# Layer 2 of a four-layer graph network: row sums behind out's kept sum, statistics of x behind the keys' store, loads of x written a block sooner

## The chip, the core and the metric

The kernel runs on one core of a Trainium2 chip. A core has five engines that run side by side, each with its own queue of instructions: TensorE (PE in the profile) multiplies matrices, VectorE (DVE), ScalarE (ACT) and GpSimd (POOL) do elementwise work, and SyncE (SP) issues the transfers between the large memory and the core's on-chip buffers. An engine takes its instructions in the order in which they stand; where an operand is not ready, the engine waits. The metric is the device time of one execution in microseconds (us).

## The reference, cut to what matters

128 graphs of 64 nodes with 512 features pass four layers of the form x = x + layer(relu(layernorm(x))). The change is in layer 2, which is attention over the nodes of one graph with 8 heads of 64 features, its scores multiplied by twice the adjacency:

```python
def layer2(x, adj, Wq, bq, Wk, bk, Wv, bv, Wo, bo):
    h = maximum(layernorm(x), 0)
    q, k, v = (heads(h @ W.T + b) for W, b in ((Wq, bq), (Wk, bk), (Wv, bv)))
    scores = einsum('bhqd,bhkd->bhqk', q, k) * 64 ** -0.5
    attn = softmax(scores * (adj + adj), axis=-1)
    ctx = einsum('bhqk,bhkd->bhqd', attn, v)
    return x + merged(ctx) @ Wo.T + bo
```

Layer 1 adds its value bias to x; the kernel leaves that to the beginning of layer 2, where each block of x gets `b1v` added once.

## The kernel before

All 8192 tokens are cut into 32 blocks of 256 tokens (`T`), four graphs each. Layers 0 and 1 run interleaved, two blocks at a time, and write x to the large memory as `x1`; layer 2 then runs over all blocks and writes `x2`; layer 3 runs last. All arithmetic is 32-bit floating point. Every product of a block with a 512x512 weight matrix is made by a Strassen-like scheme (`Product`) of seven products of halves instead of eight. The class gathers them in two PSUM banks, `ab` and `dc`, in two steps: four products in `first` and `second`, three in `late`. Between the steps the intermediate sums must be saved, because the late products are added to the same banks: `keep_ab` copies `a` on ACT (`p1`) and adds `b + p1` on DVE (L281, the kept sum `u2`, `self.kept`), and `keep_dc` copies `c` on ACT (`p5`). PE can't start the late products on `ab` before the kept sum is made. The sums of halves of the input that the scheme needs are made on POOL by `sums` (L216 to L219: S1, S2, S4, S3).

One block of layer 2 takes these steps. `prepare2` loads x and the adjacency, adds `b1v` (L906), and calls `norm`: statistics on DVE (L167, L168, L170), the power -1/2 on POOL (L172), a last factor on DVE (L174) and the normalised h on ACT (L179). `turned2` transposes h on PE (L190); DVE and ACT copy it out (L195, L193). `layer2_in` makes q and k side by side, and `store_T` writes them with their bias (L310, L313, L319 on DVE, L323 on ACT, L326 on POOL). `layer2_scores` makes the scores (L642) and on DVE the product with the adjacency (L652), the row maximum (L661) and the difference (L662), then the exponential on ACT (L665), the row sums and their reciprocals on DVE (L667, L668), and the division as a multiplication on POOL (L669). `layer2_turned` transposes e on PE (L682), `layer2_context` multiplies it with v (L703) and adds the value bias, giving cT (L711 on DVE, L716 on ACT). `out_part` makes the sums of cT and the last product, which `add_to` adds to x (L335 to L342).

The loop over blocks is written as a software pipeline: in iteration b stand the products q and k of block b + 1, then the context and the last product of block b, with the scores of block b + 1 between. `prepare2(b + 2)` is called in the middle.

The order on each engine is not that of the text alone. A scheduler goes through the program with an estimate of its own and issues what it takes to be ready, the earlier in the text first; it also decides when a buffer's slot is free. `tc.issue_after(ins)` tells it not to issue the instructions inside before `ins`. The pools set how far it can run ahead: x has 4 slots, the adjacency 3, h 6, the exponentials 3. `behind[0]` is an instruction on POOL behind which the chores are put. A chore (L99) is one of the sums of weight quarters for a coming product (1.3 us each), spread over the blocks.

Of the kernel before, what the change touches and what calls it, by code (L numbers as in the profile page):

```python
# [25 lines left out]
def kernel(ctx: ExitStack, tc: tile.TileContext, a: dict, out: bass.AP):  # L26
# [7 lines left out]
    nc = tc.nc  # L34
    x_d, adj_d, adjT_d = a["x"], a["adj"], a["adjT"]
    n_tok = x_d.shape[0]
    n_blk = n_tok // T
# [164 lines left out]
    behind = [None]  # L202

    def sums(hT, name: str, places=("S", "S")):

        A11, A12, A21, A22 = (
            hT[:, j * 2 : (j + 1) * 2, i * P : (i + 1) * P] for i in range(2) for j in range(2)
        )
        (S1, S2), (S3, S4) = (
            (s[:, 0], s[:, 1])  # L210
            for s in (
                med.tile([P, 2, 2, P], FP, tag=tag, name=f"S{i}_{name}", bufs=6 if tag == "S" else 3)
                for i, tag in enumerate(places)
            )
        )
        nc.gpsimd.tensor_tensor(S1, A21, A22, ALU.add)  # L216
        nc.gpsimd.tensor_tensor(S2, S1, A11, ALU.subtract)
        nc.gpsimd.tensor_tensor(S4, A12, S2, ALU.subtract)
        behind[0] = nc.gpsimd.tensor_tensor(S3, A11, A21, ALU.subtract)  # L219
        return {1: (A11, B11), 4: (A22, T4), 5: (S1, T1), 6: (S2, T2),  # L220
                2: (A12, B21), 3: (S4, B22), 7: (S3, T3)}

    class Product:
# [84 lines left out]
        def store_T(self, y, bias):  # L308

            nc.vector.tensor_tensor(self.u3, self.b, self.p1, ALU.add)  # L310
            for m in range(2):
                f = slice(m * P, (m + 1) * P)
                nc.vector.scalar_tensor_tensor(  # L313
                    y[:, m, P:], self.d[:, f], bias[:, m : m + 1], self.u3[:, f],
                    ALU.add, ALU.add,
                )
            for m in range(2):
                f = slice(m * P, (m + 1) * P)
                nc.vector.scalar_tensor_tensor(  # L319
                    y[:, 2 + m, :P], self.c[:, f], bias[:, 2 + m : 3 + m], self.u2[:, f],  # L320
                    ALU.add, ALU.add,
                )
                nc.scalar.activation(  # L323
                    y[:, m, :P], self.a[:, f], AF.Identity, bias=bias[:, m : m + 1]
                )
            nc.gpsimd.tensor_tensor(  # L326
                y[:, 2:, P:],
                self.u3.rearrange("p (m q) -> p m q", m=2),
                self.p5.rearrange("p (m q) -> p m q", m=2),
                ALU.add,  # L330
            )
# [266 lines left out]
    def setup2():  # L598
# [5 lines left out]
            later(w)  # L604
        return made

    def layer2_in(b: int, hT, between=()):

        ops = sums(hT, f"2_{b}")
        qk = big.tile([P, 2, K, T], FP, tag="qk", name=f"qk_{b}")  # L610
        side_by_side(*(
            (ops, w, bias, lambda p, i=i, bias=bias: p.store_T(qk[:, i], bias), f"{'qk'[i]}2_{b}")
            for i, (w, bias) in enumerate(zip(made1[5], (b2q, b2k)))
        ), between=between)
        return qk, ops
# [12 lines left out]
    def layer2_scores(b: int, adjq, qk):  # L628

        ss = [
            ps_sc.tile([P, TT, hq // 2, 2, N], FP, tag="sc", name=f"s2_{b}_{o}") for o in range(2)
        ]
        for t in range(TT):
            for c in range(hq):
                for g in range(2):
                    tok = slice(t * P + g * N, t * P + (g + 1) * N)
                    for par in range(2):
                        f = slice(par * N, (par + 1) * N)  # L640
                        half = par ^ (c % 2)
                        nc.tensor.matmul(  # L642
                            ss[c % 2][half * N : (half + 1) * N, t, c // 2, g, :],
                            qk[f, 0, c, tok], qk[f, 1, c, tok],
                            start=True, stop=True,
                        )
        es = []
        for o in range(2):

            e = med.tile([P, TT, hq // 2, 2, N], FP, tag="e2", name=f"e2_{b}_{o}", bufs=3)  # L650
            eh = e.rearrange("p t c g j -> p (t c g) j")
            nc.vector.tensor_tensor(  # L652
                e.rearrange("p t c g j -> p t c (g j)"),
                ss[o].rearrange("p t c g j -> p t c (g j)"),
                adjq.rearrange("p t g j -> p t (g j)")
                .unsqueeze(2)
                .to_broadcast([P, TT, hq // 2, 2 * N]),
                ALU.mult,
            )
            mx = small.tile([P, TT * hq], FP, tag="mx2", name=f"mx2_{b}_{o}")  # L660
            nc.vector.tensor_reduce(mx, eh, AX.X, ALU.max)  # L661
            nc.vector.tensor_tensor(  # L662
                eh, eh, mx.unsqueeze(2).to_broadcast([P, TT * hq, N]), ALU.subtract
            )
            nc.scalar.activation(e, e, AF.Exp, scale=0.25)  # L665
            r = small.tile([P, TT * hq], FP, tag="r2", name=f"r2_{b}_{o}")
            nc.vector.tensor_reduce(r, eh, AX.X, ALU.add)  # L667
            nc.vector.reciprocal(r, r)  # L668
            nc.gpsimd.tensor_tensor(  # L669
                eh, eh, r.unsqueeze(2).to_broadcast([P, TT * hq, N]), ALU.mult  # L670
            )
            es.append(e)
        return es

    def layer2_turned(b: int, es):
        pTs = []
# [220 lines left out]

    loaded2, normed2 = {}, {}

    def prepare2(b: int):  # L900
        if b < n_blk:
            loaded2[b] = load_x(b, x1[b], 2), load_adjq(b)

            for t in range(TT):
                x = loaded2[b][0]
                nc.vector.tensor_tensor(x[:, t, :], x[:, t, :], b1v, ALU.add)  # L906
            normed2[b] = norm(x, f"2_{b}")
# [13 lines left out]
    next(setup)  # L921
    open_end = []
    for i, (layer, b) in enumerate(steps):
        if i == 1:
            made1 = next(setup)
        between = [[], [chore], []]
        for n, end in open_end:
            between[n].append(end)
        if i + 1 < len(steps):
            between[0].append(lambda: prepare(i + 1))  # L930
            between[2].append(lambda: turned(i + 1))
        else:
            between[0].append(lambda: prepare2(0))
            between[2].append(lambda: turned2(0))
        if layer == 0:
            softmax = layer0(b, *loaded[b], *normed[i], between)
            open_end = [(0, lambda b=b, softmax=softmax: layer0_end(b, *softmax))]
        else:
            attention = layer1(b, *loaded[b], *normed[i], between)
            open_end = [  # L940
                (1, lambda b=b, a=attention: layer1_end(b, loaded[b][0], *a, x1[b]))
            ]
        if i == len(steps) - 3:
            made2 = setup2()

# [30 lines left out]
    coming = values(0, ops)  # L976
    next(coming)
    es = layer2_scores(0, loaded2[0][1], qk)
    v = next(coming)
    chore(2)  # L980
    for i in (2, 1):
        w3[i] = fetched(f"L3_Wk{i}", 1 + i, nc.sync)
        later(w3[i])
    for b in range(n_blk):
        x = loaded2[b][0]
        with tc.issue_after(behind[0].ins):
            for t in range(TT):
                nc.gpsimd.tensor_tensor(x[:, t, :], x[:, t, :], made2[1], ALU.add)
        stages = iter(())
        if b == n_blk - 2:  # L990
            stages = layer3_in(0, *normed3, made_in)
            next(stages)
        if b + 1 < n_blk:
            qk, ops = layer2_in(b + 1, normed2[b + 1], [[], [lambda: chore(1 if b else 2)]])
        else:
            parts = layer3_step(0, False)
            next(parts)
            chore(2)
        if b == n_blk - 2:
            w3[0] = fetched("L3_Wk0", 4, nc.sync)  # L1000
            later(w3[0])
        pTs = layer2_turned(b, es)
        if b + 1 < n_blk:
            prepare2(b + 2)
            coming = values(b + 1, ops)
            next(coming)
        else:
            next(parts)
        cT = layer2_context(b, v, pTs)
        part = out_part(b, x, cT)  # L1010
        if b + 1 < n_blk:
            es = layer2_scores(b + 1, loaded2[b + 1][1], qk)
            v = next(coming)
            turned2(b + 2)
            next(stages, None)
        else:
            next(parts)
        side_by_side(part)
        chore(2 if b == n_blk - 2 else 0)
        nc.sync.dma_start(tokens(x2[b]), x)  # L1020
        if b == n_blk - 4:
            made3 = setup3()
        if b >= n_blk - 3:
            normed3 = layer3_norm(b - n_blk + 3, x2[b - n_blk + 3])
# [69 lines left out]
```

## Time and profile before

| what | us |
|---|---|
| median of three runs | 2693.18 |
| lowest and highest of them | 2690.39 and 2693.68 |
| the profiled execution | 2690.4 |
| its span, from the first to the last instruction | 2688.6 |
| layers 0 and 1 | 0 to about 1026 |
| layer 2, from its first q to the last out | about 1020 to 1990 |
| layer 3 | about 1960 to the end |

The span is what all lines of the trace refer to; 1.8 us lie around it. A line of a timeline gives the start, the duration, the engine, the line of the code, the operation, the output and the inputs, and how many equal instructions it merges; in brackets is the idle time of the engine before it and what ended this idle time. Durations of matmuls are modelled with their way through the pipeline and overlap, so the distance from one start to the next is what counts there. A line of the costliest groups gives the count, then the busy time, the mean of one in nanoseconds, and the idle time before. In a table of stretches the columns are the stretch, its length, and the busy time and count of PE, of the weight loads, of DVE, ACT and POOL, then PE's granted clock, the transfers' share and GB/s.

### The profile page before, as it was taken

The numbers are of one execution on the slowest core, as the hardware profiler recorded it, in microseconds if no ns is written. First come the engines' busy times: TensorE is split into PE (matmuls) and PEld (weight loads), VectorE is DVE, ScalarE is ACT, GpSimd is POOL, SyncE is SP. The second block draws the span as 40 slices with busy tenths as digits, with TensorE's granted clock in tenths as the row PEclk, the third lists the DMA queues.
The fourth block names the chain that finished last, engine by engine and source line by source line (L and its number), as shares of the span: only waits on it lengthen the run. The fifth ranks groups of instructions, "written<-read, shape, count | busy, mean of one in ns | idle before, by whom it ended". The sixth has DMA issues, their size and how long they took to land.

```text
span 2688.6 us, 52721 instructions
## 1 busy us (share of the span) xinstructions
PE 2646.6 (98%) x20752; PEld 2256.7 (84%) x20752; DVE 1682.3 (63%) x4398; ACT 942.7 (35%) x2290; POOL 1274.9 (47%) x1585
## 2 busy tenths in 40 slices
PE   8999999999999999999999999999999999999999
PEld 5888888888888888898999999999877777777776
DVE  5566666666666666555655655555666666666664
ACT  2333334333433333333333333333323333333332
POOL 3443333333334344655654565555564544444454
PEclk9999999999999999999999999999999999999999
DMA  4200111111101112111111111111211111111110
GB/s 155 69 35 34 34 34 35 42 43 37 47 34 34 34 66 78 37 52 37 39 45 44 39 37 52 37 39 52 72 50 46 56 51 51 51 51 51 51 50 32
DMA packets 103165, 129.81 MB, mean 48 GB/s; under 512 B 40834, under 2 KB 50050, under 8 KB 102916
## 3 DMA queue, kind: packets, MB, share of 16 engines
q1 hardware_dynamic: 102340, 125.38, 14.0%
q8 instruction: 163, 2.67, 0.4%
q10 hardware_dynamic: 576, 1.05, 0.1%
q14 instruction: 86, 0.70, 0.1%
HBM read 76.07 MB, written 50.34 MB: 47 GB/s over the span
## 4 chain that ended last, share of the span: by engine, by line
PE 77%; DVE 11%; DMA 5%; POOL 3%; ACT 2%; issue 2%; POOLq 0%; SPq 0%; ACTq 0%; DVEq 0%
PE ab_v L251 10%; PE ab_y L251 10%; PE dc_v L251 8%; PE dc_y L251 7%; PE ab_g L244 4%; PE ab_g L251 4%; DMA x<-x 4%; PE dc_g L244 3%; PE ab_q L244 3%; PE dc_g L251 3%; PE ab_k L244 3%; PE po L392 3%; PE tr L190 3%; PE dc_k L244 2%; PE dc_q L244 2%; DVE e L662 2%
## 5 line engine op out<-in xcount | busy, mean ns | idle before, releaser
L179 ACT ACTIVATE h<-x,nmr,rstd 128x512 f32<-128x512 f32 x256 | 194.4, 806 | 212.7 <-DVE nmr L174 208.8
L167 DVE BATCH_NORM_STATS2 stats<-x 128x6 f32<-128x512 f32 x256 | 167.3, 675 | 75.4 <-DMA x<-x 71.1
L172 POOL TENSOR_TENSOR rstd<-ve,neghalf 128x2 f32<-128x2 f32 x128 | 89.5, 699 | 260.8 <-DVE ve L170 260.5
L251 PE MATMUL ab_y<-L_Wk,hT 128*128 128x256 f32 x768 | 206.2, 391 | 3.6 <-DVE u_y L303 2.6
L251 PE MATMUL ab_v<-L_Wv,hT 128*128 128x256 f32 x768 | 202.8, 387 | 4.8 <-DVE stats L167 3.7
L251 PEld LDWEIGHTS ab_y<-L_Wk,hT 128*128 128x128 f32 x768 | 136.1, 190 | 75.9 <-issue 25.1
L251 PE MATMUL ab_v<-L_Wv,S 128*128 128x256 f32 x768 | 198.0, 381 | 0.0
L251 PE MATMUL ab_y<-L_Wk,S 128*128 128x256 f32 x768 | 197.9, 380 | 0.0
L251 PE MATMUL dc_v<-L_Wv,S 128*128 128x256 f32 x768 | 197.3, 380 | 0.0
L251 PE MATMUL dc_y<-L_Wk,S 128*128 128x256 f32 x768 | 193.8, 381 | 0.2 <-DVE u_y L851 0.2
L251 PEld LDWEIGHTS dc_y<-L_Wk,S 128*128 128x128 f32 x768 | 146.2, 191 | 21.4 <-DVE u_y L851 1.7
L251 PEld LDWEIGHTS ab_v<-L_Wv,S 128*128 128x128 f32 x768 | 146.8, 191 | 19.9
L872 POOL TENSOR_TENSOR tz<-tz,y 128x512 f32<-128x512 f32 x63 | 91.3, 1449 | 146.1 <-ACT tz L869 146.1
L251 PEld LDWEIGHTS dc_v<-L_Wv,S 128*128 128x128 f32 x768 | 143.8, 191 | 18.8 <-issue 0.8
L251 PEld LDWEIGHTS ab_y<-L_Wk,S 128*128 128x128 f32 x768 | 144.1, 191 | 18.1
L251 PEld LDWEIGHTS ab_v<-L_Wv,hT 128*128 128x128 f32 x768 | 136.5, 191 | 22.9 <-ACT qk L323 7.5
L190 PE MATMUL tr<-ident,h 128*128 128x128 f32 x1024 | 134.3, 275 | 0.4 <-ACT h L179 0.4
L190 PEld LDWEIGHTS tr<-ident,h 128*128 128x128 f32 x1024 | 119.4, 142 | 11.2 <-ACT h L179 0.8
L216 POOL TENSOR_TENSOR S<-hT 128x256 f32<-128x256 f32 x128 | 100.8, 788 | 38.4 <-ACT hT L193 36.0
L326 POOL TENSOR_TENSOR qk<-u_q,p_q 128x256 f32<-128x256 f32 x32 | 23.3, 727 | 195.5 <-DVE u_q L310 195.5
L281 DVE TENSOR_TENSOR u_v<-ab_v,p_v 128x256 f32<-128x256 f32 x96 | 40.6, 423 | 109.7 <-ACT p_v L280 109.7
L219 POOL TENSOR_TENSOR S<-hT 128x256 f32<-128x256 f32 x128 | 107.0, 836 | 1.2
(238 smaller groups left out, 6472.6 us busy)
## 6 DMA issues: line engine op xcount, KB each, us to landing
x<-x SPq DMA_DIRECT2D x128, 512.0 KB, 3.4
x<-in_x_dram SPq DMA_DIRECT2D x32, 512.0 KB, 3.5
out_dram<-x SPq DMA_DIRECT2D x31, 512.0 KB, 2.8
adjT<-in_adjT_dram SPq DMA_DIRECT2D x64, 64.0 KB, 1.9
adjq<-in_adj_dram SPq DMA_DIRECT2D x64, 64.0 KB, 2.3
L_Wk<-in_L_Wk_dram SPq DMA_DIRECT2D x16, 256.0 KB, 5.2
L_Wv<-in_L_Wv_dram SPq DMA_DIRECT2D x12, 256.0 KB, 5.1
q<-in_L_Wqk_dram ACTq DMA_DIRECT2D x4, 256.0 KB, 5.4
```

The source lines that it names most:

```text
L167: nc.vector.bn_stats(stats[:, t, :], x[:, t, :])
L172: nc.gpsimd.tensor_tensor(rstd, ve, neghalf, ALU.pow)
L179: nc.scalar.activation(h, x[:, t, :], AF.Relu, bias=nmr[:, t : t + 1], scale=rstd[:, t : t + 1])
L190: nc.tensor.transpose(pt[:, k, :], h[:, k * P : (k + 1) * P], ident)
L216: nc.gpsimd.tensor_tensor(S1, A21, A22, ALU.add)
L219: behind[0] = nc.gpsimd.tensor_tensor(S3, A11, A21, ALU.subtract)
L244: nc.tensor.matmul(dst[:, m * P : (m + 1) * P], w[:, place, k, m * P : (m + 1) * P], left[:, k, :], start=key not in self.begun, stop=last ...
L251: nc.tensor.matmul(dst, left[:, k, :], w[:, place, k, :], start=key not in self.begun, stop=last and k == 1, skip_group_check=True,)
L281: self.kept = nc.vector.tensor_tensor(self.u2, self.b, self.p1, ALU.add)
L392: nc.tensor.matmul(ps[t][half[g ^ t]], e[half[g], t, :], us[t][half[g]], start=True, stop=True)
L662: nc.vector.tensor_tensor(eh, eh, mx.unsqueeze(2).to_broadcast([P, TT * hq, N]), ALU.subtract)
L872: nc.gpsimd.tensor_tensor(tz[t], tz[t], y0[:, t, :], ALU.add)
```

## The change

Three groups of edits, all in the order of layer 2's work; no instruction is added or removed.

*Row sums.* The row sums, their reciprocals and the multiplication leave `layer2_scores` and become `layer2_divided`. For block 0 it is called directly behind the scores. For the others it is called behind the last product, and nothing of it is issued before that product's kept sum.

*Statistics and sums.* `store_T` keeps two of its instructions: `taken`, the last of its DVE instructions (L319), and `stored`, the addition on POOL (L326). `prepare2(b + 2)` is issued after `taken` of the keys of block b + 1. In `layer2_in` the sums of a block are issued after `stored` of the keys of the block before (for block 0, after `behind[0]`), and after block 0's scores `behind[0]` is set to its `stored`.

*Loads.* The loads of x and of the adjacency move from `prepare2` to `fetch2`, which is called one block sooner: `fetch2(b + 3)` beside `prepare2(b + 2)`, and for blocks 0 to 2 within the last steps of layers 0 and 1.

```diff
-                nc.vector.scalar_tensor_tensor(
+                self.taken = nc.vector.scalar_tensor_tensor(
                     y[:, 2 + m, :P], self.c[:, f], bias[:, 2 + m : 3 + m], self.u2[:, f],
...
-            nc.gpsimd.tensor_tensor(
+            self.stored = nc.gpsimd.tensor_tensor(
                 y[:, 2:, P:],
...
+    of_qk = {}
+
     def layer2_in(b: int, hT, between=()):
 
-        ops = sums(hT, f"2_{b}")
+        with tc.issue_after((of_qk[b - 1][1].stored if b else behind[0]).ins):
+            ops = sums(hT, f"2_{b}")
         qk = big.tile([P, 2, K, T], FP, tag="qk", name=f"qk_{b}")
-        side_by_side(*(
+        of_qk[b] = side_by_side(*(
...
             nc.scalar.activation(e, e, AF.Exp, scale=0.25)
+            es.append(e)
+        return es
+
+    def layer2_divided(b: int, es):
+
+        for o, e in enumerate(es):
+            eh = e.rearrange("p t c g j -> p (t c g) j")
             r = small.tile([P, TT * hq], FP, tag="r2", name=f"r2_{b}_{o}")
             nc.vector.tensor_reduce(r, eh, AX.X, ALU.add)
             nc.vector.reciprocal(r, r)
             nc.gpsimd.tensor_tensor(
                 eh, eh, r.unsqueeze(2).to_broadcast([P, TT * hq, N]), ALU.mult
             )
-            es.append(e)
-        return es
...
+    def fetch2(b: int):
+        if b < n_blk:
+            loaded2[b] = load_x(b, x1[b], 2), load_adjq(b)
+
     def prepare2(b: int):
         if b < n_blk:
-            loaded2[b] = load_x(b, x1[b], 2), load_adjq(b)
...
+        if i == len(steps) - 2:
+            fetch2(0)
...
         else:
+            fetch2(1)
             between[0].append(lambda: prepare2(0))
...
+            if b == n_blk - 2:
+                open_end.append((1, lambda: fetch2(2)))
...
     es = layer2_scores(0, loaded2[0][1], qk)
+    layer2_divided(0, es)
     v = next(coming)
+    behind[0] = of_qk[0][1].stored
...
         if b + 1 < n_blk:
-            prepare2(b + 2)
+            with tc.issue_after(of_qk[b + 1][1].taken.ins):
+                prepare2(b + 2)
+            fetch2(b + 3)
...
-        side_by_side(part)
+        (of_o,) = side_by_side(part)
+        if b + 1 < n_blk:
+            with tc.issue_after(of_o.kept.ins):
+                layer2_divided(b + 1, es)
```

## The prediction, made before the changed kernel had run

> **What bounds the kernel now.** I read the page's busy table first, then the sums over stretches, then the timelines of TensorE, DVE and POOL inside layer 2.
>
> ```profile
> span 2688.6 us, 52721 instructions
> PE 2646.6 (98%) x20752; PEld 2256.7 (84%) x20752; DVE 1682.3 (63%) x4398; ACT 942.7 (35%) x2290; POOL 1274.9 (47%) x1585
> ...
> 1061.42:1826.05 764.63, 754.06 (x8114) 699.12 (x8113) 431.52 (x1058) 263.73 (x674) 425.44 (x527) 1.00 0.13 42
> ```
>
> PE sets the time: it never rests long, so only what removes a PE wait counts. The stretch holds 26 blocks of layer 2, 764.63 / 26 = 29.41 us each. An undisturbed block (transposes of e at 1417.31 to those at 1446.41) takes 29.10, so 764.63 - 26 x 29.10 = 8.0 us are occasional stalls. Inside every block there is one more, at out's late products:
>
> ```profile
> 1429.98 1.03 PE L251 MATMUL dc_o<-L_Wo,cT 128*128 128x256 f32 x4
> 1430.84 0.38 PE L244 MATMUL dc_q<-S,L_Wq 128*128 128x128 f32 x2
> 1431.43 1.13 PE L251 MATMUL ab_o<-L_Wo,cT 128*128 128x256 f32 x4 [0.21 <-DVE u_o L281]
> 1432.40 1.03 PE L251 MATMUL ab_o<-L_Wo,S_c 128*128 128x256 f32 x4
> ...
> 1428.33 1.26 DVE L667 TENSOR_REDUCE r<-e 128x8 f32<-128x512 f32 x2
> 1429.52 0.31 DVE L668 RECIPROCAL r<-r 128x8 f32<-128x8 f32 x2
> ...
> 1430.97 0.41 DVE L281 TENSOR_TENSOR u_o<-ab_o,p_o 128x256 f32<-128x256 f32 x1
> ```
>
> Read starts, not durations. Two dc_q matmuls fill in and are worth 0.22 (8 take 0.89), so PE should go on at 1431.06, but starts at 1431.43: 0.37 lost. Its first group then takes 0.97 to the next start where others take 0.87: 0.10 more. It waits for the kept sum u_o, which ends at 1431.38, behind the row sums on DVE. The occasional stalls begin with a load of x, and the entry into layer 2 has its own:
>
> ```profile
> 1090.09 1.29 DVE L906 TENSOR_TENSOR x<-x,L_bv 128x512 f32<-128x512 f32 x2 [4.74 <-DMA x<-x]
> ...
> 1093.02 1.13 PE L251 MATMUL ab_v<-L_Wv,hT 128*128 128x256 f32 x4 [1.46 <-DVE stats L167]
> ...
> 1044.13 0.48 PE L642 MATMUL s<-qk 64*64 64x64 f32 x16 [3.54 <-POOL qk L326]
> 1044.54 2.01 PE L251 MATMUL ab_v<-L_Wv,hT 128*128 128x256 f32 x4
> 1046.35 1.87 PE L251 MATMUL ab_v<-L_Wv,S 128*128 128x256 f32 x4
> 1048.05 1.03 PE L251 MATMUL dc_v<-L_Wv,S 128*128 128x256 f32 x4
> ```
>
> DVE stands at L906 for a load that has just been issued; everything behind it on DVE (storing q and k) is late, and in turn PE. At the entry the last store of k (L326) sits on POOL behind four sums of the next block and a weight chore (1038.50 to 1042.91).
>
> [...] after the 3.54 us wait two groups take 1.81 and 1.70 from start to start, against 0.97 and 0.87, 1.67 us on top. [...] L218, which meets the subtraction L662, takes half as long again as L217.
>
> ```profile
> L218 POOL TENSOR_TENSOR S_c<-cT,S_c 128x256 f32<-128x256 f32 x32 | 35.4, 1106 | 2.4
> L217 POOL TENSOR_TENSOR S_c<-S_c,cT 128x256 f32<-128x256 f32 x32 | 23.3, 727 | 0.0
> ```
>
> **The change part by part.** I compared the order in which the two built programs' instructions stand on each engine. PE's order differs only in the filler: it moves behind out's late products, its work unchanged. SP's order is the same but for single places at the entry and exit. In the old order too the load of x(n+4) follows the store of x(n), because the scheduler had pulled loads and statistics ahead of the written order. So the loads do not come sooner. What changes is their use: beside the products q, k of block 12 stood the bias and statistics of x(14), now x(13), whose load was issued a block (29 us) earlier.
>
> *Loads' wait.* The load takes 2.8 us behind the store plus some 3.5 us; with 29 us to spare no wait remains: -8.0. Bounds: 0 (another cause) and -8.0. I take -8.0: the longest stalls, at 1093.02, 1212.07, 1359.83 and 1477.27, all name the statistics L167, with L906 held by the DMA before them.
>
> *Entry.* The sums of block 1 now follow the stores of q and k on POOL, and L906 of x(2), x(3) with their statistics are off DVE there. The k store can run at about 1036 and the scores' last 16 matmuls follow the first 48. Gain 3.54 + 1.67 = 5.2. What is late next: POOL then does two chores (1.27 each) and two additions of bo (1.25 each), 5.0 us, so S1 of block 1 is there at 1041.8; PE, 3.5 us earlier, asks at 1043.4. Bounds -3 and -5.6; I take -5.2.
>
> *Row sums behind the kept sum.* 1.26 + 0.31 us leave DVE's path to u_o. They cost nothing later: DVE next waits for out's late products (2.09 us before L337 in a neighbouring block), and the multiplication on POOL, now behind L336, ends near 5 us after out's late start, where the transposes of e come at 15.1. The price is behind it on POOL: L338, L342 and the store of x come about 1 us later; its load has a block to spare. Full gain 0.37 + 0.10 = 0.47 less the rounding in the sum below: PE's block without the wait is 14 groups of L251 at 0.866, 14 of L244 at 0.893, two transposes at 0.875, 0.98 and 1.11 for the 64-wide products and 0.19 for two switches = 28.66, that is 0.44 less than 29.10.
>
> *Statistics behind the keys' store.* This adds a chain that must end inside the block. Time from out's late start: dc_k ends 15.10; DVE stores k until 16.35 (L313 follows by 0.21, then 2 x 0.52); L906 1.22, two L167 1.20, aggregates, u_v (0.33) and ve: 19.5; POOL's power and nmr 1.0: 20.4. The v sum u_v lies in this queue: 19.25, needed at 21.6. h on ACT 20.6 to 22.0; the transposes want it at 24.3: 2.3 spare. But cT's four activations now queue behind h: they end at 23.2, where they were done 1.4 us after pc and are now 2.7 after. POOL's sums of cT begin at 23.2, the third (S2) ends at 25.3 undisturbed and, as it now meets L662 (from 24.0), up to 26.2. PE needs S2 at 26.06. L662 ends at 26.5 instead of 25.9, u_o at 28.5, needed at 28.66. So the block is closely fitted: a new wait of 0 to 0.35 per block. I take 0.1, so 0.33 x 28 blocks = -9.2; bounds -12.3 and +2.
>
> *Exit.* Bias and statistics of x(31) (L906, L167: 2.4 us) and of layer 3's first block (another 1.5) now share one block, ahead of cT on DVE, and one L780 (0.68) stands before u_o: 1 to 1.5 us late once or twice. I take +2, bounds 0 and +4.
>
> Sum: -8.0 - 5.2 - 9.2 + 2 = -20.4. The profiled execution took 2690.4 (span 2688.6 and 1.8 around it), so 2670.0. The median of the three runs is 2693.2, 2.8 above it, which I count into the range.
>
> **Rivals.** (1) *Tight fit takes the steady gain*: S2 or u_o late by 0.4 in each block. For: a gap of only 0.1 to 0.8 us by my working. Against: today's S2 is done 1.9 us before its use. -8.0 - 5.2 + 0 + 2 = -11.2: 2679. (2) *No new wait at all and a clean exit*: -8.0 - 5.2 - 12.3 + 0 = -25.5: 2665. (3) *The loads' stalls stay*, as SP's order is unchanged: -5.2 - 9.2 + 2 = -12.4: 2678. Against: the block that is used is another. (4) *Slower*: the chain k store, statistics, h, cT, S2 ends late in every block and PE waits at ab_o<-S_c. It decides from 25.5 - 2 = 23.5 us over 28 blocks = 0.84 us of wait per block; at 1.2 us it gives +10: 2700. For: all four engines stand in this chain[...]. Against: my sum would have to be wrong by 0.8 us or more.
>
> **How the numbers follow.** Forecast (2664 to 2675) 0.50; rival 2 beyond it 0.09; rivals 1 and 3 together (2675 to 2685) 0.26; between that and no change 0.06; slower 0.09. A difference under 0.2% (5.4 us) can hardly be told from no change here. The range leaves out the slow cases and the far end of rival 2: 2662 to 2684. Faster 0.86, same 0.05, slower 0.09.
>
> **What would show it.** Right: the wait of ab_o for u_o gone from PE's list; transposes of e 28.7 to 28.9 us apart, evenly from the second block on; L906 without a DMA wait; scores of block 0 in one run of 64. Wrong: waits of ab_o<-S_c for POOL L217, or of the late ab_o still for u_o, in most blocks; a stop before the transposes of h for ACT; a wait over 3 us left between 1035 and 1050.

## The result and the profile after

| what | before | after |
|---|---|---|
| median of five runs, us | 2690.39 | 2680.69 |
| lowest and highest, us | 2689.22 and 2693.68 | 2679.86 and 2683.20 |
| ratio of after to before, with its 95% interval | | 0.9959 (0.9948 to 0.9971) |
| span of the profiled execution, us | 2688.6 | 2678.1 |

The change saves about 10 us, half of the 20.4 that were forecast. The first lines of the page of the changed kernel are the span and the busy time, share and instructions of each engine:

```profile
span 2678.1 us, 52780 instructions
...
PE 2639.5 (99%) x20752; PEld 2253.1 (84%) x20752; DVE 1702.8 (64%) x4398; ACT 947.7 (35%) x2290; POOL 1288.7 (48%) x1585
```

PE has the same 20752 instructions and still sets the time. Where the time went is read from the starts of the transposes of e, one group per block of layer 2. Before, those of block 0, 28 and 31 start at 1061.42, 1884.26 and 1976.38. The sums over these two stretches, before:

```profile
1061.42:1884.26 822.84, 811.85 (x8739) 752.88 (x8738) 465.39 (x1141) 284.40 (x726) 457.89 (x567) 1.00 0.13 42
1884.26:1976.38 92.12, 91.80 (x910) 80.42 (x909) 57.90 (x151) 31.85 (x80) 54.74 (x67) 1.00 0.20 66
```

And after, with the first stretch divided at block 8 (columns as before: length, then busy time and count of PE, weight loads, DVE, ACT and POOL, then PE's granted clock, the transfers' share and GB/s):

```profile
1055.28:1288.06 232.78, 231.11 (x2498) 214.84 (x2497) 138.38 (x328) 82.95 (x209) 141.02 (x169) 1.00 0.13 42
1288.06:1860.61 572.55, 572.55 (x6242) 535.70 (x6241) 345.92 (x820) 207.46 (x521) 328.90 (x401) 1.00 0.13 43
1860.61:1964.74 104.13, 94.93 (x911) 82.75 (x909) 65.87 (x160) 34.65 (x85) 57.20 (x67) 0.97 0.18 58
```

The middle row has PE busy for its whole length: 20 blocks of 28.63 us without one wait. The first has eight blocks of 29.10, those in which POOL still makes a chore. The last, the exit of layer 2, has 9.2 us of rest and a granted clock of 0.97; it is 12.0 us longer than the same work before. The account by stretch (the entry counts from the last product with v of layer 1's block 30, at 1012.26 before and 1011.60 after):

| stretch | before, us | after, us | difference |
|---|---|---|---|
| layers 0 and 1 (no part of the change) | | | -0.7 |
| entry, to the first transposes of e | 49.2 | 43.7 | -5.5 |
| 28 blocks: stalls over 29.10 each | 8.0 | 0 | -8.0 |
| 28 blocks: 8 of 29.10, 20 of 28.63 | 814.8 | 805.3 | -9.5 |
| exit, blocks 29 to 31 | 92.1 | 104.1 | +12.0 |
| from there to the end | 712.2 | 713.4 | +1.1 |

The sum is -10.6 with rounding, against -10.5 in the spans. PE's timeline after shows each of them (start, duration, and in brackets the wait before):

```profile
1038.38 1.21 PE L645 MATMUL s<-qk 64*64 64x64 f32 x64
1039.52 1.13 PE L251 MATMUL ab_v<-L_Wv,hT 128*128 128x256 f32 x4
...
1105.34 1.16 PE L244 MATMUL ab_k<-hT,L_Wk 128*128 128x128 f32 x8 [0.21 <-DVE x L341]
...
1415.26 1.03 PE L251 MATMUL dc_o<-L_Wo,cT 128*128 128x256 f32 x4
1416.12 1.03 PE L251 MATMUL ab_o<-L_Wo,cT 128*128 128x256 f32 x4
1416.98 1.03 PE L251 MATMUL ab_o<-L_Wo,S_c 128*128 128x256 f32 x4
...
1885.90 2.80 PE L754 MATMUL pu<-w3vT,aw 128*2 128x512 f32 x4 [2.58 <-DMA w3vT<-in_L_WvT_dram]
...
1912.87 1.13 PE L251 MATMUL ab_o<-L_Wo,cT 128*128 128x256 f32 x4 [1.47 <-DVE u_o L281]
...
1920.93 0.77 PE L400 MATMUL sm_i<-di,ones_bd 128*128 128x128 f32 x2 [3.41 <-DVE di L793]
1921.49 1.91 PE L244 MATMUL ab_q<-S,L_Wq 128*128 128x128 f32 x8
...
1964.74 1.06 PE L690 MATMUL tr<-ident,e 128*128 128x128 f32 x8 [1.73 <-ACT hT L193]
```

The scores of block 0 are one run of 64 and full rate follows. At 1415 to 1417 the late products of out follow each other by 0.86 without the filler and without the wait for u_o. In blocks 1 to 8 there is a small wait (0.21) for L341, which empties the last PSUM bank of out's product. At the exit there are four waits that the kernel before didn't have, and after the long one PE runs at half rate (granted clock 0.50 from 1920.85 to 1924.26; 1.70 from 1921.49 to the next start, where 0.89 is usual). Against before, block 29 takes 4.0 us more (37.09), block 30 6.4 (35.83) and block 31 1.6 (31.21). The first wait is explained by SP's timeline. After:

```profile
1866.32 0.37 SPq L744 DMA_DIRECT2D w3vT<-in_L_WvT_dram  x1
1880.66 0.36 SPq L1043 DMA_DIRECT2D x<-x  x1
1881.11 0.42 SPq L744 DMA_DIRECT2D w3vT<-in_L_WvT_dram  x1
```

Before (one row for both loads):

```profile
1889.96 13.13 SPq L736 DMA_DIRECT2D w3vT<-in_L_WvT_dram  x2
1903.77 0.37 SPq L1020 DMA_DIRECT2D x<-x  x1
```

Both loads of layer 3's w3vT stood ahead of the store of x2 of block 28; now the second one stands behind it. The third wait is explained by DVE's timeline of block 30:

```profile
1911.50 0.97 DVE L788 SCALAR_TENSOR_TENSOR hu<-h,u 128x512 f32<-128x512 f32 x1
...
1912.40 0.41 DVE L281 TENSOR_TENSOR u_o<-ab_o,p_o 128x256 f32<-128x256 f32 x1
...
1919.98 0.42 DVE L341 TENSOR_TENSOR x<-dc_o,x 128x256 f32<-128x256 f32 x1 [1.61 <-POOL x L338]
1920.32 0.46 DVE L793 TENSOR_TENSOR di<-eye,sij 128x128 f32<-128x128 f32 x1
```

One hu of layer 3's block 0 stands before u_o, three more follow the row sums, and di, which PE needs, stands behind L341, which waits 1.61 for POOL. The fourth wait names ACT's copy of hT; on DVE the statistics of layer 3's block 2 (L167) stand 2.88 us for their load just before it, and the wait is gone in the runs that move these statistics (e8 to e11).

### The profile page after: what moved, and what is told of

The parts are those of the page before. It is cut to its first block, busy times and chain, and to the rows that moved or that the text cites. A ratio compares the mean times of both kernels' runs of the same rounds, so it can differ in the third digit from the quotient of the medians.

```text
span 2678.1 us, 52780 instructions
## 1 busy us (share of the span) xinstructions
PE 2639.5 (99%) x20752; PEld 2253.1 (84%) x20752; DVE 1702.8 (64%) x4398; ACT 947.7 (35%) x2290; POOL 1288.7 (48%) x1585
## 4 chain that ended last, share of the span: by engine, by line
PE 81%; POOL 6%; DVE 5%; DMA 4%; ACT 3%; issue 2%; ACTq 0%; POOLq 0%; SPq 0%; DVEq 0%
PE ab_v L251 11%; PE ab_y L251 9%; PE dc_v L251 8%; PE dc_y L251 6%; PE ab_g L244 4%; PE ab_k L244 4%; PE ab_g L251 4%; PE ab_q L244 4%; PE tr L190 3%; PE dc_g L244 3%; PE dc_g L251 3%; PE po L392 3%; PE dc_k L244 3%; PE ab_o L251 3%; PE dc_q L244 3%; DMA x<-x 2%
## 5 line engine op out<-in xcount | busy, mean ns | idle before, releaser
L172 POOL TENSOR_TENSOR rstd<-ve,neghalf 128x2 f32<-128x2 f32 x128 | 89.8, 701 | 365.6 <-DVE ve L170 365.4
L167 DVE BATCH_NORM_STATS2 stats<-x 128x6 f32<-128x512 f32 x256 | 165.3, 677 | 74.6 <-DMA x<-x 68.4
L190 PEld LDWEIGHTS tr<-ident,h 128*128 128x128 f32 x1024 | 119.5, 142 | 10.5
L306 POOL TENSOR_TENSOR gv<-u_g,p_g 128x256 f32<-128x256 f32 x32 | 23.4, 730 | 174.4 <-DVE u_g L303 174.4
L217 POOL TENSOR_TENSOR S<-S,hT 128x256 f32<-128x256 f32 x128 | 101.0, 789 | 11.6 <-DVE ve L170 10.3
```

Of the source, the lines that this page charges most:

```text
L167: nc.vector.bn_stats(stats[:, t, :], x[:, t, :])
L172: nc.gpsimd.tensor_tensor(rstd, ve, neghalf, ALU.pow)
L190: nc.tensor.transpose(pt[:, k, :], h[:, k * P : (k + 1) * P], ident)
L306: nc.gpsimd.tensor_tensor(y[:, 1, F:], self.u3, self.p5, ALU.add)
```

## The experiments

Each row is a kernel of its own, timed beside the kernel before in the same set of runs; the changed kernel itself has 0.9959 (0.9948 to 0.9971).

| run | median, us | ratio to before (95% interval) |
|---|---|---|
| e1 row sums back | 2692.84 | 1.0001 (0.9992 to 1.0010) |
| e2 statistics' tie undone | 2719.71 | 1.0099 (1.0084 to 1.0114) |
| e3 statistics of x(31) elsewhere | 2672.14 | 0.9922 (0.9907 to 0.9937) |
| e4 w3vT ahead of the store | 2672.64 | 0.9926 (0.9910 to 0.9943) |
| e5 entry's ties undone | 2677.10 | 0.9944 (0.9930 to 0.9959) |
| e6 additions exchanged | 2682.74 | 0.9964 (0.9952 to 0.9976) |
| e7 chores behind the store of k | 2683.53 | 0.9970 (0.9957 to 0.9982) |
| e8 exit mended | 2672.75 | 0.9930 (0.9915 to 0.9944) |
| e9 exit mended otherwise, entry's ties undone | 2672.51 | 0.9925 (0.9911 to 0.9939) |
| e10 e9 and the exchange | 2673.56 | 0.9928 (0.9915 to 0.9940) |
| e11 all, the exchange in blocks 0 to 11 | 2662.02 | 0.9888 (0.9873 to 0.9903) |
| e12 loads written as before | 2679.04 | 0.9948 (0.9931 to 0.9965) |

**e1: the row sums back in front of the kept sum.**

```diff
             es = layer2_scores(b + 1, loaded2[b + 1][1], qk)
+            layer2_divided(b + 1, es)
             v = next(coming)
...
-        if b + 1 < n_blk:
-            with tc.issue_after(of_o.kept.ins):
-                layer2_divided(b + 1, es)
```

> The changed kernel with the row sums, their reciprocal and the multiplication put back in front of the kept sum of out (statistics and loads stay as changed). Theory (steady gain is the kept sum no longer waiting, the exit loss has three separate sources): the wait of ab_o for u_o is back in every block, all blocks 29.1 us apart, so +0.47 x 20 = +9.4; the second load of w3vT stands ahead of the store of x2 of block 28 again, so block 29 loses its wait (-2.6 and about -3 of half rate); block 30 keeps most of its loss, since bias and statistics of x(31) still share a block with those of layer 3's block 0: 2680.7 + 9.4 - 5.5 = about 2684 (2682 to 2687). Rival A (the exit loss comes as a whole from the later row sums, whose multiplication holds the addition that di stands behind): exit as before the change, -12: 2678. Rival B (tight fit eats most of the steady gain): about 2676.

All of the gain is gone, more than any of the three forecasts said. PE's timeline of this kernel:

```profile
1422.83 1.13 PE L251 MATMUL ab_o<-L_Wo,cT 128*128 128x256 f32 x4 [0.57 <-DVE u_o L281]
...
1936.08 0.46 PE L400 MATMUL sm_i<-di,ones_bd 128*128 128x128 f32 x2 [2.92 <-DVE di L793]
```

The wait for u_o is 0.57 here, where it was 0.2 in the kernel before, and blocks are 29.46 us apart, not 29.10. So with the statistics behind the keys' store, the chain to u_o is longer, and the row sums in it cost 0.83 per block (29.46 less 28.63). The rest was as the theory had it: block 29 takes 33.1 (as before the change, with both loads of w3vT ahead), block 30 still 35.7 with 2.92 of wait for di, so the later row sums are not the main thing that makes di late.

**e2: bias and statistics not tied to the keys' store.**

```diff
-            with tc.issue_after(of_qk[b + 1][1].taken.ins):
-                prepare2(b + 2)
+            prepare2(b + 2)
```

> The changed kernel without the tie of bias and statistics of x to the keys' store (row sums and loads as changed). Theory: DVE again stands at the bias for a load just issued, the stalls worth 8.0 us are back, and blocks 30 and 31 return to 29.4 and 29.6 (-8.0), block 29 keeps the wait for w3vT: 2680.7 + 8.0 - 8.0 = 2681 (2678 to 2684), with waits L917 <-DMA in the trace. Rival A (calling the loads a block sooner is what removed the stalls): no DMA wait, 2673. Rival B (the exit loss has nothing to do with the statistics): 2689.

This is 27 us slower than the kernel before, and 39 us above what the theory gave. DVE stands for the load again, but it did so in the kernel before too, in all 28 blocks. The lists of DVE's waits over blocks 0 to 28 (in all, times, longest) have, before and here:

```profile
DVE x L906 <- DMA x<-x: 78.3, 28, 4.7
...
DVE x L917 <- DMA x<-x: 92.2, 28, 5.4
```

What such a wait costs PE is new. PE's list over the same blocks of this kernel has two entries:

```profile
PE pc L711 <- ACT pT L694: 19.8, 54, 0.8
PE ab_v L251 <- DVE stats L167: 9.6, 10, 2.1
```

The second is the old stall, which the kernel before had 4 times (3.7 us). The first, in 27 blocks out of 28, it didn't have, and ACT's timeline of one block shows its cause. Here:

```profile
1613.71 0.81 ACT L179 ACTIVATE h<-x,nmr,rstd 128x512 f32<-128x512 f32 x1 [1.10 <-DVE nmr L174]
1614.43 1.05 ACT L694 COPY pT<-tr 128x512 f32<-128x512 f32 x2
```

Before:

```profile
1419.14 1.07 ACT L686 COPY pT<-tr 128x512 f32<-128x512 f32 x2
1420.36 1.52 ACT L179 ACTIVATE h<-x,nmr,rstd 128x512 f32<-128x512 f32 x2
```

In this order one h stands on ACT in front of the copies of the transposed e, and h waits for the statistics, which wait for the load. No run tells how much of it this order on ACT makes alone. The waits for the load are longer too: the row sums' later multiplication makes out's additions on POOL late. From the start of u_o to the end of L341 it is 6.9 us here (1413.51 to 1420.44) and 5.6 before (1430.97 to 1436.56). In the changed kernel, where the multiplication stands at the same late place, SP issues the store of x 7.4 us after u_o's start (1422.64 less 1415.24), before 5.9 (1436.82 less 1430.97), and the load that reuses its buffer 2.8 behind the store in both. The entry's gain is gone too: first transposes at 1062.85, with waits of 2.05 and 3.08 for u_v. The two main parts of the change need each other: either alone gives nothing or loses.

**e3: only x(31)'s bias and statistics moved.**

```diff
-            with tc.issue_after(of_qk[b + 1][1].taken.ins):
+            at = of_o.kept if b == n_blk - 3 else of_qk[b + 1][1].taken
+            with tc.issue_after(at.ins):
                 prepare2(b + 2)
```

> Only bias and statistics of x(31) move: behind the kept sum of out of block 28 instead of the keys' store of block 30. Theory (two blocks' statistics in one block delay cT, e, u_o and di): waits of ab_o for u_o (1.47) and of sm_i for di (3.41, and the half rate after it) go, blocks 30 and 31 come to 29 to 30 us: -7 (-5 to -8), 2674. Rival A (the multiplication behind the kept sum makes sm_i late, through the addition L338 on which the DVE instruction ahead of di waits): only -1 to -2, 2679.

The theory held, 8.5 us by the medians and 7.5 by the spans: the waits of 1.47 and 3.41 are gone and block 30 takes 28.85 instead of 35.83. Blocks 29 and 31 are a little longer (38.07 and 32.49). Block 29 has, on PE's timeline:

```profile
1885.95 3.49 PE L754 MATMUL pu<-w3vT,aw 128*2 128x512 f32 x4 [3.57 <-DMA w3vT<-in_L_WvT_dram]
```

**e4: only the store of x2 of block 28 moved behind both loads of w3vT.**

```diff
-        nc.sync.dma_start(tokens(x2[b]), x)
         if b == n_blk - 4:
             made3 = setup3()
+            with tc.issue_after(made_in.pop().ins):
+                nc.sync.dma_start(tokens(x2[b]), x)
+            made_in.clear()
+        else:
+            nc.sync.dma_start(tokens(x2[b]), x)
```

(`setup3` puts its two load instructions into `made_in`.)

> Only the store of x2 of block 28 moves, behind both loads of w3vT on SP's queue. Theory (PE's 2.58 us wait at pu and the half rate after it come from the order on SP): block 29 falls from 37.1 to about 31.5, -5.5: 2675 (2674 to 2678). Rival A (the load waits for its buffer, which PE frees at the same time anyway): -1 or less, 2680. Rival B (what block 29 gains, block 30 loses again, as its statistics set the end): 2679 to 2681 with block 30 longer.

The wait is gone (PE's timeline of this kernel, the same four products; 1.88 instead of 2.80 as well):

```profile
1882.24 1.88 PE L754 MATMUL pu<-w3vT,aw 128*2 128x512 f32 x4
```

Block 29 falls to 32.82, 4.3 less. The waits of 1.47 and 3.41 in block 30 stay, as they should. Block 31 loses 1.0 of it again, and 2.5 more come behind the exit, where a wait for a weight chore (1.16 in the changed kernel, at 1969.55) is gone: 5.9 by the spans, 8 by the medians.

**e5: the two ties at the entry undone.**

```diff
-        with tc.issue_after((of_qk[b - 1][1].stored if b else behind[0]).ins):
-            ops = sums(hT, f"2_{b}")
+        ops = sums(hT, f"2_{b}")
...
-    behind[0] = of_qk[0][1].stored
```

> Only the two ties at the entry are undone (sums of block 1 and the chores and additions of bo may again stand in front of the store of k of block 0 on POOL); everything from block 1 on stays as changed. Theory (the entry's gain is POOL's place): the scores of block 0 wait again for POOL L326 by 3 to 5 us, with the half rate after it, first transposes of e about 5.5 us later: 2686 (2685 to 2689). Rival A (the entry gained because bias and statistics of x(2), x(3) left DVE): no wait, 2681.

The theory fell. POOL again has sums and two chores in front of the store of k (L326), yet the scores of block 0 are one run of 64, and the first transposes of e come 43.13 us after the last product of layer 1's block 30 (1056.81 less 1013.68), not later than in the changed kernel (1055.28 less 1011.60, 43.68). POOL's timeline of this kernel:

```profile
1035.10 0.73 POOL L216 TENSOR_TENSOR S<-hT 128x256 f32<-128x256 f32 x1 [0.80 <-ACT hT L193]
...
1037.95 2.51 POOL L99 TENSOR_TENSOR L_Wo<-L_Wo 128x512 f32<-128x512 f32 x2
1040.41 0.74 POOL L326 TENSOR_TENSOR qk<-u_k,p_k 128x256 f32<-128x256 f32 x1
```

The sums start at 1035.1 as their operand is there, and L326 ends just in time. In the kernel before they began at 1038.5; DVE's and ACT's timelines of that kernel show what their operand, hT, stood behind:

```profile
1029.31 1.29 DVE L906 TENSOR_TENSOR x<-x,L_bv 128x512 f32<-128x512 f32 x2 [4.75 <-DMA x<-x]
...
1036.44 1.52 ACT L179 ACTIVATE h<-x,nmr,rstd 128x512 f32<-128x512 f32 x2 [0.53 <-DVE nmr L174]
1037.86 0.56 ACT L193 COPY hT<-tr 128x512 f32<-128x512 f32 x1
```

DVE stood for a load, its statistics came late, and ACT copied hT out behind the h that waited for them. With e2 this says that the entry's gain comes from the bias and statistics of x(2) and x(3), which no longer stand at that place; the ties add nothing.

**e6: two additions exchanged.** DVE adds the PSUM bank (L341) first, and POOL adds the kept sum (L338) after it.

```diff
-            nc.gpsimd.tensor_tensor(x[:, 1, :F], self.u3, x[:, 1, :F], ALU.add)
             nc.vector.tensor_tensor(x[:, 0, F:], self.c, x[:, 0, F:], ALU.add)
             nc.vector.tensor_tensor(x[:, 0, :F], self.a, x[:, 0, :F], ALU.add)
             nc.vector.tensor_tensor(x[:, 1, :F], self.d, x[:, 1, :F], ALU.add)
+            nc.gpsimd.tensor_tensor(x[:, 1, :F], self.u3, x[:, 1, :F], ALU.add)
```

> Only the order of two additions into the same quarter of x changes: DVE adds the PSUM bank first (L341), POOL adds the kept sum after it (L338), so that DVE no longer waits for POOL. Theory (in blocks 1 to 8 PE's wait at ab_k is the PSUM bank held until L341, which stands behind a chore and the multiplication on POOL; in block 30 di stands behind the same L341): distances of the first eight blocks fall from 29.10 to 28.63 (-3.8), and sm_i's wait of 3.41 loses 1.6 and its half rate (-3): 2674 (2672 to 2677). Rival A (POOL as such is full in blocks with a chore, and another of its results is late instead): 2680 with a new wait of PE in these blocks.

The mechanism is right and the time is not. All 28 blocks take 28.63, 3.8 us less over the first eight. In block 30 the wait for di falls from 3.41 to 2.05, and the block takes 32.88, 2.95 less. But the store of x2 of block 28 is later, and the load of w3vT behind it too: block 29 takes 40.63, 3.5 more. Behind the first transposes of block 31 6.0 us more are lost, with a wait of 4.02 for POOL's L172 in the statistics of layer 3's block 2, for whose x DVE stands 7.04 (2.88 in the changed kernel). PE's timeline of block 29:

```profile
1885.24 3.57 PE L754 MATMUL pu<-w3vT,aw 128*2 128x512 f32 x4 [5.49 <-DMA w3vT<-in_L_WvT_dram]
```

**e7: the chores moved behind the store of k.**

```diff
-            qk, ops = layer2_in(b + 1, normed2[b + 1], [[], [lambda: chore(1 if b else 2)]])
+            qk, ops = layer2_in(b + 1, normed2[b + 1], [[], []])
+            chore(1 if b else 2, of_qk[b + 1][1].stored)
```

(`chore` takes the instruction to stand behind.)

> Only the chores of layer 3's weights move: from behind the sums of q and k to behind the store of k. Theory (a chore of 1.27 us ahead of the multiplication is what makes the bank late in blocks 1 to 8): all blocks 28.63, -3.8: 2677, exit unchanged. Rival A (a chore there stands ahead of rstd, makes h and cT late, and PE waits for S_c): 2681 or more. Rival B (blocks 1 to 8 are slow for another reason): 29.10 stays, 2681.

Rival A. The waits for L341 are gone, so the chore's old place made them, but blocks with a chore take 29.40, worse than 29.10, and PE's timeline names the sum of cT:

```profile
1185.47 1.13 PE L251 MATMUL ab_o<-L_Wo,S_c 128*128 128x256 f32 x4 [0.51 <-POOL S_c L217]
```

A chore takes 1.27 us of POOL. It costs 0.77 here (29.40 less 28.63, of which 0.51 is the wait shown) and 0.47 in its old place: the chain from the keys' store over h and cT to S_c has no 1.27 us to spare.

**e8 to e11: the exit mended, and the whole.** e8 has the edits of e3 and e4, and the statistics of layer 3's block 2 behind the copy of hT of its block 1 on DVE:

```diff
-                nc.vector.tensor_copy(ht, pt)
+                turns.append(nc.vector.tensor_copy(ht, pt))
...
-            normed3 = layer3_norm(b - n_blk + 3, x2[b - n_blk + 3])
+            if b == n_blk - 1:
+                with tc.issue_after(turns[-1].ins):
+                    normed3 = layer3_norm(2, x2[2])
+            else:
+                normed3 = layer3_norm(b - n_blk + 3, x2[b - n_blk + 3])
```

> The exit alone is mended: bias and statistics of x(31) behind the kept sum of block 28, the store of x2 of block 28 behind both loads of w3vT, statistics of layer 3's block 2 behind the copies of hT of its block 1. Theory (the exit's loss is made of these separate waits and they add up): blocks 29, 30, 31 at about 32.5, 28.9 and 29.5, together 91 instead of 104.1, -13: 2668 (2665 to 2671). Rival A (the waits overlap, what one edit gains is waited for elsewhere): no better than one of the edits alone, 2672.

Blocks 29 to 31 fall from 104.1 to 93.4, but 3.7 us come back after them (waits of 1.74 at den and 2.40 at pc), as rival A said; no better than e3 or e4. e9 puts x(31)'s statistics behind the kept sum of q of block 30, those of layer 3's block 2 behind a reciprocal (L847), and leaves the entry's ties out (the diff is against e8):

```diff
-            at = of_o.kept if b == n_blk - 3 else of_qk[b + 1][1].taken
+            at = of_qk[b + 1][0].kept if b == n_blk - 3 else of_qk[b + 1][1].taken
...
-                turns.append(nc.vector.tensor_copy(ht, pt))
+                nc.vector.tensor_copy(ht, pt)
...
-        nc.vector.reciprocal(r, r)
+        turns.append(nc.vector.reciprocal(r, r))
```

> The exit mended once more, and the entry's two ties left out as in the run without them: bias and statistics of x(31) behind the kept sum of q of block 30 (where DVE waits nearly 10 us for the key product), the store of x2 of block 28 behind both loads of w3vT, statistics of layer 3's block 2 behind the reciprocal of the weights' sum of its block 0. Theory (what the first mended exit left are waits made by where the two statistics were put: 1.17 at ab_q, 1.74 at den, 2.40 at pc): these go, -4 to -5 against the first mended exit, and one chore done earlier saves about 1 more: 2667 (2664 to 2669). Rival A (the time comes back as waits of layer 3's blocks 1 and 2 for their statistics): 2671 to 2674.

Again only moved: blocks 29 to 31 take 92.0, and PE waits 1.80 for cT of block 31 and 2.33 for S_c, since these statistics now stand in front of cT. e10 adds the exchange of e6, with the same diff.

> The same, and also the exchanged additions (DVE's from the PSUM bank ahead of POOL's). Theory: blocks 1 to 8 come to 28.63 as in the run of the exchange alone (-3.8), and since the store of x2 of block 28 now follows the loads of w3vT, the wait of 5.49 us that the exchange alone had there does not come: 2663 (2661 to 2666). Rival A (the later POOL addition makes the store and the loads of layer 3's blocks late, and the exit takes the gain): 2667 or more.

Rival A: the first eight blocks come to 28.63 (3.6 less than in e9), blocks 29 to 31 take 96.0, 3.9 more than in e9, and 3.2 more are lost behind them. e11 keeps the exchange to blocks 0 to 11 and moves the statistics of layer 3's block 2 behind cT:

```diff
-        def add_to(self, x):
+        def add_to(self, x, bank_first):
...
-            nc.gpsimd.tensor_tensor(x[:, 1, :F], self.u3, x[:, 1, :F], ALU.add)
+            if not bank_first:
+                nc.gpsimd.tensor_tensor(x[:, 1, :F], self.u3, x[:, 1, :F], ALU.add)
...
+            if bank_first:
+                nc.gpsimd.tensor_tensor(x[:, 1, :F], self.u3, x[:, 1, :F], ALU.add)
```

(`turns[-1]` is now the addition that makes cT, L719; `add_to` is called with `b < 12`.)

> The second mended exit and entry, with the statistics of layer 3's block 2 behind cT of block 31 (they stood before it and made it late by 1.80 and 2.33), and with the additions exchanged in blocks 0 to 11 alone, away from the exit. Theory: against the run of the second mended exit -3.8 from blocks 1 to 8 and -4 from the two waits: 2665 (2663 to 2668). Rival A (the exit keeps its own bound and gives the waits back elsewhere): 2669 or more.

2662.02, just under the forecast's 2663 to 2668 and better than both kernels: 30 us under the kernel before and, by the ratios, 0.7% under the changed one. The sums over layer 2's blocks 0 to 28 and over its exit:

```profile
1056.75:1858.29 801.54, 801.54 (x8738) 749.94 (x8737) 484.15 (x1148) 290.42 (x729) 469.42 (x569) 1.00 0.13 43
1858.29:1950.20 91.91, 91.33 (x910) 80.58 (x909) 63.75 (x154) 32.91 (x83) 57.64 (x68) 1.00 0.20 66
```

PE does not rest once in 28 blocks, and the exit takes 91.9, what it took before the change.

**e12: the loads of x written where they stood.**

```diff
+            if b: fetch2(b + 2)
             with tc.issue_after(of_qk[b + 1][1].taken.ins):
                 prepare2(b + 2)
-            fetch2(b + 3)
```

> The loads of x are written in the order of before again (x(b+2) beside its statistics, not x(b+3)); row sums and statistics stay as changed. Theory (the load follows the store that frees its buffer, wherever it is written; the statistics' later place alone removed the stalls): the order on SP and the distances of the blocks are the same, 2681 (2679 to 2683). Rival A (the sooner load removed the stalls): DVE L917 waits for DMA again in many blocks, 2688 or more.

The same time within the intervals, the same blocks (29.09 and 28.63), and no wait of L917 for a load in these blocks. Beside the other two parts this one does nothing.

## Why the prediction was half right

*Loads' wait, -8.0.* It is 8.0: the stalls over 29.10 came to 822.84 less 28 times 29.10, and after the change there are none. The cause stood in the prediction: not the load's place, which SP's order doesn't change (e12), but the later use (without it, in e2, the waits for the statistics are back).

*Entry, -5.2.* It is 5.5, but half for the wrong reason. The wait named POOL L326, and the prediction took POOL's order as what had to change. e5 has the old order there and no wait: the sums had been late because their operand was, behind an h on ACT that waited for the statistics on DVE.

*Row sums, -9.2.* It is 9.5, from errors that cancel, which is luck. A block without a wait was worked out as 28.66 and is 28.63, and the new wait of 0.1 in every block isn't there (3.6 us more gain in 28 blocks). In their place eight blocks lose the whole 0.47 (3.8), because a chore and the multiplication (1.26 and 2.05 us on POOL, at 1098.82 and 1102.09) stand before L338 and L341 holds a PSUM bank that k's product wants (e6 and e7 take this wait away). The prediction said that L338 would come about 1 us later and counted the store of x as its only follower; the bank was the other.

*Exit, +2, bounds 0 and +4.* This step failed: it is +12.0. The sentence counted only DVE's queue before u_o ("1 to 1.5 us late once or twice"), and that part is right (1.47, once). It left out three followers. SP's order differed at single places at the exit, which the prediction mentions and prices at nothing; one of them puts the second load of w3vT behind a store, 2.58 us of wait and slow products after it (2.80 instead of 1.88), 4.3 by e4. And di, which PE waits for, stands in the same DVE queue behind two blocks' statistics: 3.41 and the half rate after it; with the 1.47 that is 7.0 in block 30, gone when the statistics of x(31) stand elsewhere (e3). The multiplication on POOL, through L341, is a part of it: with the row sums in front the wait is still 2.92 (e1), without L341's wait 2.05 (e6). The third are the statistics of layer 3's block 2, with 1.73 of wait in block 31, which takes 1.6 more. None of the three was in the bounds of this step. The other three terms came within 0.4 us of their forecasts, so this one is nearly the whole miss: the time lies outside the forecast of 2664 to 2675, and the wide range of 2662 to 2684 holds it only because it reached as far as the rivals.

*The rivals.* The result lies where a part of the gain is lost, but not by rival 1's wait in each block, and not by rival 3, whose stalls are gone. Rival 4, the chain to S_c, doesn't decide; e7 shows that it is near: 1.27 us more on POOL brings it.

## What to carry to other kernels

When an order of instructions changes, price the first and last blocks of a stage by their own queues, SP's too: a swapped transfer and two statistics in one block cost here more than the steady part gained. A wait's named releaser is the last link; ask what made it late, and test parts singly, since here neither of two parts gave anything alone. Mend an exit link by link with the next wait in view: two repairs that gave 8 us each gave no more together (e3, e4, e8), because the wait moved on, and the gain came when the last one had a free place (e11).

## What the runs showed of the hardware

PE's half rate didn't follow the length of its rest. The four products with w3vT took 2.80 after rests of 2.58 (the changed kernel) and 2.20 (e7), and 1.88, as without a rest (e4), after 2.23 (e12): rests of nearly the same length, with and without a slower clock. From the start of these four to that of the same ab_k<-S products it is 4.66 in e7 (1889.96 to 1894.62) and 3.02 in e12 (1886.47 to 1889.49), so the slower clock cost 1.6 us (block 29 takes 36.70 in e7 and 35.11 in e12).

In the changed kernel the granted clock is 0.50 from 1886.71, from 1920.85 and from 1999.35, each time for 3.41 us. Stretches of the same length around the rest before w3vT, of e7 and then of e12 (the first time after the length is PE's, the 1.00 or 0.50 its clock):

```profile
1887.37:1890.78 3.41, 1.21 (x6) 0.38 (x5) 0.00 (x0) 0.47 (x2) 2.58 (x3) 1.00 0.93 282
1890.78:1894.19 3.41, 3.41 (x10) 1.63 (x9) 0.00 (x0) 0.63 (x2) 0.00 (x0) 0.50 0.10 37
...
1884.65:1888.06 3.41, 1.59 (x4) 0.26 (x4) 0.00 (x0) 0.00 (x0) 1.77 (x2) 1.00 0.80 285
1888.06:1891.47 3.41, 3.41 (x29) 3.19 (x29) 0.42 (x1) 1.00 (x3) 0.00 (x0) 1.00 0.05 12
```

In e7 the first stretch holds the whole rest of 2.20, and the next has a clock of 0.50; in e12 it holds 1.82 of the 2.23, and the next has 1.00. What made the difference was not shown. The prediction looked for half rate only after the rest of 3.54 (there too the clock is 0.50, from 1044.63 for 3.4 us); e7 has it after 2.20, and e12 doesn't have it after 2.23.
